# The GELU between the expert layers: in pieces of two column tiles instead of four

## The chip, the core and the metric

The kernel runs on one NeuronCore of a Trainium2 chip. Its engines are TensorE (PE; its weight loads are listed as PEld), VectorE (DVE), ScalarE (ACT) and GpSimd (POOL); the SP queue issues most DMAs. The metric is the device time of one execution in microseconds, as the median of the runs.

## The reference

The input x has 4 sequences of 2048 tokens with 512 features. It is normalised, and the sum of three things is returned: x, a self-attention over the normalised tokens, and a mixture of experts over them.

```python
xn = _layernorm(x, axis=-1)
# attention: 16 heads of 32
qkv = jnp.einsum('bnc,dc->bnd', xn, qkv_w) + qkv_b
attn = softmax(q @ k^T * HEAD_DIM ** (-0.5))
attention = einsum('bnc,dc->bnd', attn @ v, proj_w) + proj_b
# experts: the two best of 8 for each sequence, by its first token
_, idx = jax.lax.top_k(xn[:, 0, :] @ Wr + br, 2)
h = jnp.einsum('bsd,bkde->bkse', xn, W1[idx]) + b1[idx]
h = jax.nn.gelu(h, approximate=False)
o = jnp.einsum('bkse,bkef->bksf', h, W2[idx]) + b2[idx]
out = x + attention + jnp.sum(o, axis=1) / 2
```

All of it is float32. This is shortened: reshapes and the split into heads are left out.

## The kernel before

**Units.** The attention is cut into 1024 units. A unit U is one block of 128 keys against one chunk of 512 queries, for a group of four heads; 16 units are a chunk, four chunks a group, four groups a sequence. A unit opens with the `shift` matmuls (L725), which put the negative row maxima into four PSUM banks, and goes on with the scores on top of them (`score`, L733). Between these stand the plain scores of a unit that comes 22 units later (`score_max`, L715), of which VectorE takes maxima (L855). ScalarE then takes Exp of the four score tiles into a `p` tile (L849), and GpSimd adds the `p` tiles up (`add_weights`, L762 and L766; the last of a chunk by an adding DMA, L764). An even unit also has the product of the last two `p` tiles with v (`weigh`, L745). All PSUM tiles come from one ring of 8 banks (`bank`), so a tile waits until the tile eight places before it has been read. The `p` tiles come from a ring of 4.

**Dense work.** The linear layers are cut into items, and an odd unit takes one item behind its scores: `qk` and `v` projections, `w1` and `w2` of the experts, and `proj`. `dense` emits an item; most have 32 matmuls (`product`, L485). Twenty-two further units ahead of unit 0, with negative numbers, hold the first `v` items and the first `w1` items.

**The experts.** The first layer is done for two chunks of tokens at a time with seven products of half-size blocks in place of eight, each for two halves of the columns (q = 0, 1). The order of the products in `w1` items is `GAPS`: (1,0); (1,1); (6,0),(6,1); (7,0),(7,1); (5,0),(3,0); (5,1),(3,1); (4,0),(4,1); (2,0),(2,1). `combine` adds each into the tiles `hT[0]` (the even chunk) and `hT[1]` (the odd chunk), of 128 partitions by four column tiles of 512. Columns 2q and 2q+1 of `hT[1]` are complete with product (3,q), those of `hT[0]` with (2,q). Eight `w2` items follow, four blocks of 128 tokens that read `hT[1]`, then four that read `hT[0]`. There are 16 such passes: 4 sequences, 2 pairs of chunks, 2 experts.

**The GELU.** It is done in place, by one ScalarE instruction over a whole `hT` tile, in the unit two after the item that completes it. `dense` notes it in `curves` under that unit's number, and the unit's loop takes it behind its four Exps:

```python
curve = curves.pop(U, None)
if curve is not None:
    flat = curve.rearrange("p f n -> p (f n)")
    nc.scalar.activation(flat, flat, AF.Gelu)
```

In the unit that holds a GELU, `dense` is told so (`on_dve`), and `combine` then copies a first product with VectorE instead of ScalarE.

**The planner.** `Plan` gives every odd unit its item ahead of time: fixed ones (`qk`, `v`) at places written out by hand, the others from queues in order. Some odd units stay empty; candidates are those at place 5 of a chunk, and one is left empty whenever the share owed is above zero, unless it would hold a GELU (`curve` in the planner). Loads on SP are placed from the items' units; `keys_at` makes the sum over GpSimd's totals one unit later where place 5 is empty.

Of the kernel before, what the change touches and what calls it, by code (L numbers as in the profile page):

```python
# [37 lines left out]
class Plan:  # L38
# [6 lines left out]
    def __init__(self, B, DC, NCH, NT, TPC):  # L45
# [13 lines left out]
        for G in range(1, B * DC):  # L59
            b, g = divmod(G, DC)  # L60
            first = (G - 1) * self.per_group
            for n, products in enumerate(GAPS):
                at = (11, 12, 13, 14, 15, 16, 17, 19) if g else (5, 6, 7, 8, 9, 11, 12, 13)
                fixed[first + 2 * at[n] + 1] = ("qk", b, g, products)
            if g == 0:
                at = [n for n in range(14, 32) if n % 8 != 2]
# [10 lines left out]
        for b in range(1, B):  # L77
            q1 = (b - 1) * self.per_seq + self.per_group
            q2 = q1 + self.per_group
            for k in range(TOP_K):  # L80
                at = q1 + ((NT - 1, q2 - q1 + 5 * NT - 1) if b > 1 else (-1, NT - 1))[k]
# [4 lines left out]
            for n in range(NT):  # L86
                self.extra.setdefault(q1 + 2 * (16 + n) + 1, []).append(("stats", b, n))
                c, i = divmod(n, TPC)
                at = q2 + 2 * (1 + 18 * (c // 2) + 5 * (c % 2) + i) + 1
# [3 lines left out]
            for p in range(NCH // 2):  # L93
                at = q2 + 2 * NT * (p + 1) - 1
# [46 lines left out]
        current, before, owed = [], None, 0  # L141
        for s in slots:
            if s in fixed:
                self.items[s] = [fixed.pop(s)]
                before = None
                continue
            curve = before is not None and before[0] == "w1" and before[4][-1] in ((3, 1), (2, 1))
            before = None
            if s in rests:
                owed += share  # L150
                if owed > 0 and not curve:
                    owed -= 1
                    continue
            if not current:
                for queue in (proj, ffn):
                    if queue and queue[0][0] <= s:
                        current = queue.pop(0)[1]
                        break
            if current:
                before = current.pop(0)  # L160
                self.items[s] = [before]
# [77 lines left out]
def block_kernel(  # L239
# [37 lines left out]
    def bank(name):  # L277
        return ps.tile([P, CH], F32, tag="bank", name=name)
# [202 lines left out]
    def product(pp, terms, last=True, first=True):  # L481

        for n, (lhsT, rhs) in enumerate(terms):
            for j in range(GH):
                nc.tensor.matmul(  # L485
                    pp[rows_of(j), :], lhsT[:, rows_of(j)], rhs,
                    start=(first and n == 0), stop=(last and n == len(terms) - 1),
                )

    kT, qT = {}, {}  # L490
    hT, bias, b1s = {}, {}, {}
# [16 lines left out]
    def project_v(b, n, xn, w, U):  # L508

        c, i = divmod(n, TPC)  # L510
        pp = bank(f"vps_{b}_{n}")
        product(pp, [(xn[:, d, ts(i, P)], w[:, d, :]) for d in range(DC)])
        t = pair.tile([P, D], F32, tag="vrow", name=f"v_{b}_{n}")
        nc.vector.tensor_tensor(t, pp, bv_bc, ALU.add)
        later(U + 2, lambda: nc.sync.dma_start(v_dram[b, c][:, i, :], t))

    def combine(i, x, c, b1, b2, on_dve):

        add = nc.vector.tensor_tensor
        biased = nc.vector.scalar_tensor_tensor  # L520
        if i == 1 and on_dve:
            nc.vector.tensor_copy(c[0, 0], x)
        elif i == 1:
            nc.scalar.activation(c[0, 0], x, AF.Identity)  # L524
        elif i == 6:
            add(c[0, 1], x, c[0, 0], ALU.add)
        elif i == 7:
            add(c[1, 0], x, c[0, 1], ALU.add)
        elif i == 5:
            biased(c[1, 1], x, b2, c[1, 0], ALU.add, ALU.add)  # L530
            add(c[0, 1], x, c[0, 1], ALU.add)
        else:
            at, b_ = {3: ((0, 1), b1), 4: ((1, 0), b2), 2: ((0, 0), b1)}[i]
            biased(c[at], x, b_, c[at], ALU.add, ALU.add)
# [29 lines left out]
    def blocks(kind, b, n, U):  # L564
# [10 lines left out]
        else:  # L575
# [4 lines left out]
            if n == 3:  # L580
                later(U + (2 if b == 0 else 4), lambda: nc.sync.dma_start(ws_dram[b, k], raw))

    outs = {}

    def dense(item, U, on_dve, between):
        kind, b = item[:2]
        tiles = [held[n] for n in plan.needs(item)]
        if kind == "qk":
            g, products = item[2:]
            for n, (i, p) in enumerate(products):  # L590
                wt, xt = tiles[2 * n : 2 * n + 2]
                pp = bank(f"qkps_{b}_{g}_{i}_{p}")
                product(pp, [(wt[:, d, 0, :], xt[:, d, :]) for d in range(2)])
                o = outs.setdefault((b, g, p), {})
                where = {1: (0, 0), 6: (0, 1), 7: (1, 0), 5: (1, 1)}.get(i)
                if where is not None:
                    c = 2 * p + where[1]
                    t = "kq"[where[0]]
                    o[where] = (kT if t == "k" else qT)[b, g, c] = kv_pool.tile(
                        [P, CH], F32, tag=t, name=f"{t}T_{b}_{g}_{c}",  # L600
                        bufs=2 * NCH if t == "k" else NCH + 3,
                    )
                combine(i, pp, o, bqkv[:, DC + g : DC + g + 1], bqkv[:, g : g + 1], on_dve)
                if n == 0:
                    between()
        elif kind == "v":
            n = item[2]
            project_v(b, n, tiles[1] if b else stage[0, n // TPC], tiles[0], U)
        elif kind == "w1":
            p, k, products = item[2:]  # L610
            for n, (i, q) in enumerate(products):
                wt, xt = tiles[2 * n : 2 * n + 2]
                if (i, q) in ((1, 0), (6, 0)):
                    cc = int(i == 6)
                    hT[cc] = stream.tile(
                        [P, DC, CH], F32, tag="h", name=f"h_{b}_{p}_{k}_{cc}", bufs=2
                    )
                pp = bank(f"hps_{b}_{p}_{k}_{i}_{q}")
                product(pp, [(wt[:, d, q, :], xt[:, d, :]) for d in range(2)])
                o = {(r, cc): hT[cc][:, 2 * q + r, :] for r in range(2) for cc in hT}  # L620
                cols = [b1s[b, k][:, 2 * q + r : 2 * q + r + 1] for r in range(2)]
                combine(i, pp, o, *cols, on_dve)
                if n == 0:
                    between()
                if (i, q) in ((3, 1), (2, 1)):
                    at = U + 2 if U > 0 or U == -1 else U + 1
                    curves[at] = hT[i == 3]
        elif kind == "w2":
            p, c, k, i = item[2:]
            w, row = tiles  # L630
            pp = bank(f"ops_{b}_{c}_{k}_{i}")
            product(pp, [(hT[c % 2][:, f, ts(i, P)], w[:, f, :]) for f in range(DC)])
            nc.vector.scalar_tensor_tensor(row, pp, 0.5, row, ALU.mult, ALU.add)  # L633
            later(U + 2, lambda: nc.sync.dma_start(part_dram[b, c, i], row))
        else:
            qc, i = item[2:]
            at, w, row = tiles
            pp = bank(f"prps_{b}_{qc}_{i}")
            product(pp, [(at[:, g, ts(i, P)], w[:, g, :]) for g in range(DC)])
            finish(b, qc, i, pp, row, U)  # L640

    def finish(b, qc, i, pp, row, U):
        tok = qc * CH + i * P
        nc.vector.tensor_tensor(row, pp, row, ALU.add)  # L644
        later(U + 2, lambda: nc.sync.dma_start(out[b, tok : tok + P, :], row))
# [49 lines left out]
    def place(u):  # L695
        rest, kt = divmod(u, NT)
        rest, qc = divmod(rest, NCH)
        return (*divmod(rest, DC), qc, kt)

    mx, negm, sacc, psums, sums, pT = {}, {}, {}, {}, {}, {}  # L700
    curves, waiting, ends = {}, {}, []

    def later(u, do):
        waiting.setdefault(u, []).append(do)
# [124 lines left out]
    for U in range(-LEAD, plan.units):  # L829
# [20 lines left out]
        curve = curves.pop(U, None)  # L850
# [13 lines left out]
        before = place(U - NT)[:3] if U >= NT else None  # L864
# [30 lines left out]
        for step, sb, n in plan.extra.get(U, []):  # L895
# [10 lines left out]
            else:  # L906
                c, i = divmod(n, TPC)
# [6 lines left out]
        for item in plan.items.get(U, []):  # L914
            dense(item, U, curve is not None, invert if two else lambda: None)
# [28 lines left out]
    U = plan.units  # L944
# [18 lines left out]
    for i in range(TPC):  # L963
        q = ts(i, P)
# [52 lines left out]
```

## Time and profile before

| | |
|---|---|
| median of 3 runs | 5038.61 us (5038.29 to 5046.06) |
| the profiled execution | 5042.55 us, span 5040.8 us |
| TensorE busy | 4947.0 us, 98% of the span, clock 0.997 |
| GpSimd busy | 4429.2 us, 88% |
| VectorE busy | 3740.2 us, 74% |
| ScalarE busy | 2394.0 us, 47% |
| GELU | 32 of 1.91 us |
| table loads on ScalarE | 71 of 1.28 us: 32 ahead of a GELU, 35 ahead of an Exp, 4 ahead of a square root |

Busy shares are averages over the whole execution. TensorE's matmuls overlap, and their ends are modelled, so that single instructions of about 0.6 us stand closer together than their durations say. The names in the rows are those of the program: `p`, `h` (the `hT` tiles), `s` and `m` (scores), `acc` (product with v). "<-" in square brackets names what ended the idle time before an instruction. A row of several instructions has the time from the first one's start to the last one's end.

### The profile page before, as it was taken

To read this page: it belongs to the slowest core of one execution; us is meant where nothing else is said; L and a number is where in the kernel's file an instruction comes from. 1 tells how busy PE (TensorE), PEld (TensorE's weight loads), DVE (VectorE), ACT (ScalarE), POOL (GpSimd) and SP (SyncE) were. 2 spreads that over 40 slices of the span, in tenths; PEclk is the share of its full clock that TensorE was granted. 3 is DMA by queue.
4 is the path that set the end of the run, shared out by engine and by line. 5 is a ranking of instruction groups with operands and counts; after the bars stand their busy time and mean duration, and the time that the engine had idled before them with its cause. 6 is when DMAs were issued, how large, how long until landed. Compare 5 with 4: busy or idle time off the path is not lost. (4 is left out here: it accounts for less than half of the span.)

```text
span 5040.8 us, 107883 instructions
## 1 busy us (share of the span) xinstructions
PE 4947.0 (98%) x45028; PEld 1725.8 (34%) x45028; DVE 3740.2 (74%) x5909; ACT 2394.0 (47%) x4406; POOL 4429.2 (88%) x1498
## 2 busy tenths in 40 slices
PE   8999999999999999999999999999999999999998
PEld 2333333333333333333333333333333333333332
DVE  5777887777777788777777777877777777777762
ACT  1445445454444545454444444555444445454453
POOL 2799998999898998999889998999988988999981
PEclk9999999999999999999999999999999999999999
DMA  6333334433233434434224234434423343323312
GB/s 219 111 103 117 115 96 127 142 122 109 80 107 104 126 107 122 140 114 141 89 86 125 85 121 118 146 122 136 134 70 106 100 123 101 101 80 101 107 62 95
DMA packets 297128, 568.16 MB, mean 113 GB/s; under 512 B 24636, under 2 KB 144188, under 8 KB 279744
## 3 DMA queue, kind: packets, MB, share of 16 engines
q1 hardware_dynamic: 287568, 495.19, 29.4%
q0 software_dynamic: 9072, 66.06, 6.7%
q8 instruction: 354, 5.80, 0.5%
q14 instruction: 134, 1.10, 0.1%
HBM read 367.44 MB, written 127.66 MB: 98 GB/s over the span
## 5 line engine op out<-in xcount | busy, mean ns | idle before, releaser
L766 POOL TENSOR_TENSOR psum<-psum,p 128x2048 f32<-128x2048 f32 x819 | 3722.4, 4545 | 167.6 <-ACT p L849 129.2
L849 ACT ACTIVATE p<-s 128x512 f32<-128x512 f32 x4096 | 2118.0, 603 | 2364.9 <-PE m L715 2181.8
L855 DVE TENSOR_REDUCE mx<-m 128x1 f32<-128x512 f32 x4096 | 2544.2, 684 | 570.1 <-PE m L715 569.8
L733 PE MATMUL s<-qT,kT 32*128 32x512 f32 x8192 | 1919.1, 588 | 0.0
L715 PE MATMUL m<-kT,qT 32*128 32x512 f32 x8192 | 1911.3, 590 | 6.4 <-ACT h L524 3.4
L715 PEld LDWEIGHTS m<-kT,qT 32*128 32x128 f32 x8192 | 920.9, 184 | 334.9 <-issue 244.7
L745 PE MATMUL acc<-p,v 128*32 128x512 f32 x8192 | 988.5, 600 | 37.0 <-ACT p L849 37.0
L733 PEld LDWEIGHTS s<-qT,kT 32*128 32x128 f32 x8192 | 768.6, 185 | 29.2 <-issue 7.3
L485 PE MATMUL ops<-wb_w,h 128*32 128x512 f32 x4096 | 466.0, 595 | 0.6 <-ACT p L849 0.2
L745 PEld LDWEIGHTS acc<-p,v 128*32 128x32 f32 x8192 | 214.2, 109 | 737.0 <-ACT p L849 420.5
L762 POOL TENSOR_TENSOR psum<-p,p 128x2048 f32<-128x2048 f32 x63 | 287.5, 4563 | 203.2 <-ACT p L849 203.2
L754 DVE TENSOR_TENSOR sacc<-acc,sacc 128x512 f32<-128x512 f32 x448 | 309.9, 692 | 158.3 <-PE acc L745 158.3
L485 PE MATMUL hps<-xt,wt_w 128*32 128x512 f32 x3584 | 411.0, 596 | 2.5 <-ACT p L849 2.0
L725 PE MATMUL s<-negm,ones_b 32*128 32x512 bf16 x4096 | 405.7, 385 | 6.2 <-ACT p L849 5.9
L485 PE MATMUL qkps<-xt,wt_qk 128*32 128x512 f32 x3360 | 387.8, 599 | 9.8 <-ACT p L849 9.2
L725 PEld LDWEIGHTS <-ones_b 32*128 32x128 bf16 x4096 | 103.2, 91 | 858.2 <-issue 858.1
L870 DVE RECIPROCAL sums<-sums 128x128 f32<-128x128 f32 x252 | 237.6, 943 | 0.7 <-ACT sums L784 0.7
L485 PEld LDWEIGHTS ops<-wb_w,h 128*32 128x32 f32 x4096 | 120.0, 109 | 308.6 <-issue 229.8
L633 DVE SCALAR_TENSOR_TENSOR row<-ops,row 128x512 f32<-128x512 f32 x128 | 88.4, 691 | 170.3 <-PE ops L485 116.3
L485 PE MATMUL prps<-wb_proj,xl_at 128*32 128x512 f32 x1792 | 203.9, 595 | 0.3
L485 PEld LDWEIGHTS hps<-xt,wt_w 128*32 128x32 f32 x3584 | 103.3, 109 | 268.2 <-issue 186.1
L485 PEld LDWEIGHTS qkps<-xt,wt_qk 128*32 128x32 f32 x3360 | 97.3, 110 | 273.9 <-issue 181.6
(123 smaller groups left out, 1981.6 us busy)
## 6 DMA issues: line engine op xcount, KB each, us to landing
xt<-t_dram SPq DMA_DIRECT2D x181, 512.0 KB, 4.3
xt<-xn_dram SPq DMA_DIRECT2D x133, 512.0 KB, 5.0
psum<-p POOLq DMA_DIRECT2D x63, 1024.0 KB, 8.2
part_dram<-row SPq DMA_DIRECT2D x128, 256.0 KB, 2.0
v_dram<-v SPq DMA_DIRECT2D x64, 256.0 KB, 2.7
wt_w<-ws_dram SPq DMA_DIRECT2D x128, 128.0 KB, 3.3
v<-v_dram SPq DMA_DIRECT2D x64, 256.0 KB, 4.9
row<-in_x_dram SPq DMA_DIRECT2D x64, 256.0 KB, 6.5
```

The costliest lines, as they stand in the source:

```text
L485: nc.tensor.matmul(pp[rows_of(j), :], lhsT[:, rows_of(j)], rhs, start=(first and n == 0), stop=(last and n == len(terms) - 1),)
L633: nc.vector.scalar_tensor_tensor(row, pp, 0.5, row, ALU.mult, ALU.add)
L715: nc.tensor.matmul(t, qT[b, g, qc][r, ts(i, P)], kT[b, g, kc][r, :], start=True, stop=True)
L725: nc.tensor.matmul(tiles[j], ones_b[r, :], negm[b, g, qc][r, :], start=True, stop=False)
L733: nc.tensor.matmul(tiles[j], kT[b, g, kt // TPC][r, ts(kt % TPC, P)], qT[b, g, qc][r, :], start=False, stop=True,)
L745: nc.tensor.matmul(acc[r, :], held["v", (b, g, kt // TPC)][:, (kt + n) % TPC, r], pT[u + n][:, j, :], start=(n == 0), stop=(n == 1),)
L754: nc.vector.tensor_tensor(t, acc, t, ALU.add)
L762: nc.gpsimd.tensor_tensor(psums[b, g, qc], pT[u - 1], pT[u], ALU.add)
L766: nc.gpsimd.tensor_tensor(psums[b, g, qc], psums[b, g, qc], pT[u], ALU.add)
L849: nc.scalar.activation(pT[U][:, j, :], tiles[j], AF.Exp, scale=SCALE)
L855: nc.vector.tensor_reduce(dst, t, AX.X, ALU.max, negate=True)
L870: nc.vector.reciprocal(sums[before][:, q], sums[before][:, q])
```

## The change

The GELU over a whole `hT` tile becomes two, each over two of its four column tiles, and each in an odd unit of its own. For `hT[1]` the first piece is noted when product (3,0) is done and the second when (3,1) is done. For `hT[0]` both are noted when (2,1) is done, for the next two odd units. The planner's condition for not leaving a unit empty is widened to the units that now hold a piece.

```diff
-            curve = before is not None and before[0] == "w1" and before[4][-1] in ((3, 1), (2, 1))
+            curve = before is not None and (
+                before[0] == "w1" and before[4][-1] in ((3, 0), (3, 1), (2, 1))
+                or before[0] == "w2" and before[3] % 2 == 1 and before[5] == 0
+            )
...
+    def following(U):
+
+        return U + 2 if U >= -1 else U + 1
...
-                if (i, q) in ((3, 1), (2, 1)):
-                    at = U + 2 if U > 0 or U == -1 else U + 1
-                    curves[at] = hT[i == 3]
+                if i == 3:
+                    curves[following(U)] = hT[1][:, 2 * q : 2 * q + 2, :]
+                if (i, q) == (2, 1):
+                    curves[following(U)] = hT[0][:, :2, :]
+                    curves[following(following(U))] = hT[0][:, 2:, :]
```

## The prediction

> **What bounds the kernel now.** I read the page first (busy shares and groups), then the groups with shapes kept apart, then the timeline around a GELU, on ScalarE and on TensorE, and last the waits. Times are us, of one profiled execution.
>
> The page and its groups: which engine is full, and what the GELU consists of.
>
> ```profile
> PE 4947.0 (98%) x45028; PEld 1725.8 (34%) x45028; DVE 3740.2 (74%) x5909; ACT 2394.0 (47%) x4406; POOL 4429.2 (88%) x1498
> ...
> L766 POOL TENSOR_TENSOR psum<-psum,p 128x2048 f32<-128x2048 f32 x819 | 3722.4, 4545 | 167.6 <-ACT p L849 129.2
> L849 ACT ACTIVATE p<-s 128x512 f32<-128x512 f32 x4096 | 2118.0, 603 | 2364.9 <-PE m L715 2181.8
> ```
>
> TensorE has work 98% of the time, so whatever lets it stand still is paid in full. ScalarE is idle half the time: its busy time is not what a GELU costs. The GELU's own rows, from the groups of the whole trace:
>
> ```profile
> L853 ACT ACTIVATE h<-h 128x2048 f32<-128x2048 f32 x32 | 61.2, 1912 | 0.4
> L849 ACT ACT_TABLE_LOAD x35 | 44.9, 1283 | 25.6 <-PE m L715 25.5
> L853 ACT ACT_TABLE_LOAD x32 | 41.1, 1283 | 0.6
> ```
>
> There are 32 GELUs of 1.91, and each is a detour: a load of the GELU's table before it (L853), and a load of Exp's table before the next Exp (L849; 3 of the 35 follow square roots). The L853 loads wait for next to nothing; those of L849 wait 25.5 in total for TensorE.
>
> One GELU on ScalarE, from the timeline (start, duration, engine, line, operation, idle before and releaser):
>
> ```profile
> 1718.64 2.07 ACT L849 ACTIVATE p<-s 128x512 f32<-128x512 f32 x4 [2.09 <-PE m L715]
> 1720.72 1.28 ACT L853 ACT_TABLE_LOAD   x1
> 1722.02 1.91 ACT L853 ACTIVATE h<-h 128x2048 f32<-128x2048 f32 x1
> 1724.24 1.28 ACT L849 ACT_TABLE_LOAD   x1 [0.31 <-PE m L715]
> 1725.53 2.07 ACT L849 ACTIVATE p<-s 128x512 f32<-128x512 f32 x4
> 1729.38 2.07 ACT L849 ACTIVATE p<-s 128x512 f32<-128x512 f32 x4 [1.78 <-PE m L715]
> ```
>
> And TensorE in the even unit that follows (L725 opens a unit, L745 is its product with v):
>
> ```profile
> 1722.91 0.39 PE L725 MATMUL s<-negm,ones_b 32*128 32x512 bf16 x4
> ...
> 1726.18 1.92 PE L745 MATMUL acc<-p,v 128*32 128x512 f32 x16 [1.16 <-ACT p L849]
> ...
> 1728.04 0.40 PE L725 MATMUL s<-negm,ones_b 32*128 32x512 bf16 x4
> ```
>
> The reader should see three things. First, the GELU's table load starts at 1720.72, right behind the odd unit's last Exp, and the GELU ends at 1723.93: all of it lies beside the odd unit's dense product (TensorE busy to 1722.91) and the next unit's scores. Second, Exp's table load does not follow the GELU at once. It starts at 1724.24, which is 1.33 after the unit opened. An Exp without a table load starts 1.34 after its unit opens (1729.38 against 1728.04). So the load stands behind the Exp's wait for the first scores, and its whole 1.28 falls after them. Third, TensorE then has no PSUM bank for L745 until the first Exp empties one, and is idle 1.16. The unit lasts 5.12 instead of 3.90 (one without a GELU before it: 501.41 to 505.31): 1.22 lost.
>
> That the load waits for the scores, and not for the GELU, is seen best where ScalarE has something else behind the GELU, a normalisation (L441):
>
> ```profile
> 847.55 1.28 ACT L853 ACT_TABLE_LOAD   x1
> 848.85 1.91 ACT L853 ACTIVATE h<-h 128x2048 f32<-128x2048 f32 x1
> 850.66 0.80 ACT L441 ACTIVATE xl_normal<-xl_normal,nb,sd 128x512 f32<-128x512 f32 x1
> 851.66 1.28 ACT L849 ACT_TABLE_LOAD   x1 [0.19 <-PE m L715]
> ```
>
> That unit opened at 850.33, so the load again starts 1.33 later, though the GELU had ended at 850.76, 0.90 before. Read at each of the 32 GELUs, the load starts 1.32 to 1.33 after the unit opens in 29, while their gap behind the GELU lies between 0.31 and 0.91. The 32 units behind a GELU lose 43.0 over 3.90 each: 32 x 1.22 = 39.0, and 4 more in a few where work for a new chunk or slow GpSimd sums come on top.
>
> **The change part by part.** *Removed:* 32 GELUs of 128x2048. Each held ScalarE 1.91 beside covered work. *Added:* 64 of 128x1024. Exact length unknown: at least half of 1.91 (0.96) if nothing is fixed, at most 1.91; the small rows of ScalarE (128x512 at 0.60 to 0.83) put it near 1.06. Which value is right doesn't matter. The half GELU would end some 0.85 earlier, about 1.7 before Exp's load may start at all, instead of 0.31. I count a gain of 0; what hides it is the odd unit's product and the scores. If the load could follow the GELU at once, there would be a gain, and that is the first rival.
>
> *Added, table loads:* 32 for GELU and 32 for Exp. The GELU's 1.28 starts behind the odd unit's last Exp and ends before the next unit's scores, as now: 0. Exp's 1.28 is the exposed one: 1.22 of TensorE each. Every GELU is in an odd unit and followed by an even one, so the new stalls have the place and the size of the old: 64 x 1.22 = 78.1 against 39.0, **+39.0**. The bounds for a new stall are 0 (if it falls where TensorE waits for something else anyway) and 1.6 (the longest idle before L745 behind a GELU now); I take 1.22, since 28 of 32 have the same idle of 1.16 ahead of L745.
>
> The Trainium skill speaks against this change. "ScalarE: Activation LUTs", section "Rules for kernel authors", says to do all of one table set before switching to another; "What ACT_TABLE_LOAD costs" there prices a switch at about 1283 ns plus about 1380 ns of drain, 2.66 in all. The trace has the 1283, but no drain: the load starts 0.01 after the last Exp (1720.71 to 1720.72), and the Exp 0.01 after its load. By the page, 64 new switches make 170 on ScalarE, and if half of them, Exp's, stood on the path, +85. By the row it is 1.22 for the exposed switch and 0 for the other. I take the row, which includes all that really followed a switch.
>
> *Moved:* pieces of GELU. For the odd chunk (hT[1]) the first piece goes to the unit of products (5,1),(3,1), two units earlier than before, and the second stays in that of (4,0),(4,1). For the even chunk the first stays in the unit of the first w2 block, the second goes to the second block. First readers: hT[1] is read by the first w2 block, four units after its second piece; hT[0] by the fifth, well after. So no product waits longer. GELU issues no DMA, and nothing of SP or GpSimd is passed. The half at (5,1),(3,1) runs while VectorE writes the other half of the same tile; if dependencies hold per slice, no one waits. A start-up row speaks for slices: TensorE turns the first slice of x while ScalarE still writes the later ones.
>
> ```profile
> 12.84 2.93 ACT L441 ACTIVATE x<-x,nb,sd 128x512 f32<-128x512 f32 x4 [0.85 <-POOL nb L437]
> 13.71 2.42 PEld L455 LDWEIGHTS xt<-ident,x 128*128 128x128 f32 x12 [6.11 <-ACT x L441]
> ```
>
> *Queued behind the new pieces on ScalarE:* normalisations in four of the new GELU units, 0.80 each. A half GELU ends near 5.8 after its unit opens, so the normalisation ends at 6.6, still ahead of the scores at 5.61 + 1.33 = 6.94. Cost 0. The Exps behind a load come 1.27 late, and with them GpSimd's sum of that unit. It runs 13.81 without a break over the example's stall, so it is still working off earlier units: 0. VectorE has 1.41 idle in the stalled unit: 0.
>
> *The planner:* three empty odd units (slots 53, 661, 901) now would hold a GELU piece, so each moves to the next such slot, 16 units later, and the dense items between come one odd unit earlier, with their loads on SP. The number of empty units is unchanged, and the instructions and DMAs too: 0, with a bound of 1 either way for each. The choice of engine for the copy of the first product (VectorE in a GELU unit) changes nowhere, since no first product falls into a new GELU unit.
>
> *Given back:* GpSimd, 88% busy, at times falls behind, and then Exp waits for a p buffer; the waits show it as
>
> ```profile
> ACT p L849 <- DMA psum<-p: 36.3, 9, 7.4
> ```
>
> Over the timeline, TensorE is idle 19.8 in 14 units at the third or fourth place of a chunk for this reason. A new stall shortly before lets GpSimd catch up. Six of these units have new GELUs in the 30 units before them, and at 1.22 for each such GELU and no more than is there it makes at most about 6. I take -2.
>
> *Sum:* +39.0 - 2 = +37. The profiled execution took 5042.55 (span 5040.8 and 1.75 around it), so it would be 5079.6; that execution is 3.9 above the median of the three runs (5038.61). Against the median: **5075.6**, +0.73%.
>
> **The rivals.** *The shorter GELU frees Exp's load (faster).* Place: the gap between GELU and Exp's table load. If the load were held by the GELU's end and could run before the scores, a half GELU would end at 5.8 after its odd unit opens, the load at 7.1, 1.45 after the even unit opened (5.61), so Exp is 0.12 late and not 1.27: 64 x 0.12 = 8 instead of 43, -35, about 5004. It decides from the point at which the load doesn't wait for TensorE. For it: loads and GELU fill ScalarE almost up to the scores, so the stall looks like one of length. Against: the gap, 0.31 to 0.91 at the same 1.33.
>
> *GpSimd's lag takes the stalls in.* If all 19.8 came back: +19, about 5058. For: GpSimd is second at 88%. Against: most of that lag sits away from new GELUs.
>
> *Writes wait for whole tiles.* VectorE's writes of (5,1) would wait for the half GELU, which ends at 5.8 of its unit, 1.8 behind the first product (16 matmuls from 2.05 on, 1.9 long). The queue holds 3.1 there (L530 0.74, L531 0.68, a reciprocal 0.94, L534 0.73), then the next unit's maxima, 1.9 late, of which the 1.22 stall covers part: 0.7 to 1.9 x 16 = 11 to 30 more, 5087 to 5106. Against: the slice row above.
>
> **How the numbers follow.** Chances: the stall per GELU 0.85, the freed load 0.04, GpSimd's relief 0.04, whole tiles 0.04. The load freed in about half of the cases is left 0.03; it alone ends within 0.2% (10 us, about what a measurement of this kernel tells from no change). Slower 0.93, same 0.03, faster 0.04. The range starts at 5065 (39 less twice the possible 6 of relief) and ends at 5087 (three planner moves, a few stalls of 1.6, and the 7.8 between the runs shown).
>
> **What would show it.** Right: 64 GELUs near 1.06, 64 table loads at L853 and 67 at L849; Exp's load still 1.33 after its unit opens, with a gap of about 1.2 behind the GELU; about 74 of idle ahead of L745 behind GELUs instead of 38; TensorE's busy time unchanged. Wrong: Exp's load right behind the half GELU, or even units behind a GELU under 4.5; or VectorE idle for ScalarE at L530 in the units of (5,1),(3,1).

## The result, and the profile after

The changed kernel takes 5079.66 us (median of 6 runs) against 5039.14 before, a ratio of 1.0074 (95% interval 1.0063 to 1.0086): slower by 40.5. The profiled executions, on which the readings below rest, have spans of 5078.3 and 5040.8, 37.5 apart.

The page after the change, and its groups for ScalarE and for TensorE's product with v (lines have moved on by 9: L858 is the Exp, L862 the GELU, L754 the product with v):

```profile
PE 4950.4 (97%) x45028; PEld 1731.8 (34%) x45028; DVE 3740.3 (74%) x5909; ACT 2482.9 (49%) x4502; POOL 4429.3 (87%) x1498
...
L754 PE MATMUL acc<-p,v 128*32 128x512 f32 x8192 | 987.6, 600 | 71.3 <-ACT p L858 71.3
```

```profile
L858 ACT ACT_TABLE_LOAD x67 | 86.0, 1283 | 90.6 <-PE m L724 88.7 <-issue 1.8
L862 ACT ACT_TABLE_LOAD x64 | 82.1, 1283 | 1.1
L862 ACT ACTIVATE h<-h 128x1024 f32<-128x1024 f32 x64 | 67.7, 1058 | 0.7
```

TensorE has the same number of matmuls and 3.4 more of busy time; the other 34.1 of the 37.5 is idle time. The wait ahead of the product with v, which went from 37.0 to 71.3, makes up all of it. The granted clock is 0.997 in both executions, so it does not explain the difference. On ScalarE, 64 GELUs of 1.06 take 67.7 where 32 took 61.2, and there are 64 more table loads. The idle time ahead of Exp's loads went from 25.6 to 90.6: each half GELU is done earlier, and ScalarE then stands idle until it may load the table.

One piece on ScalarE, in the same two units whose timeline was shown of before (the even unit opens at 1724.82):

```profile
1720.55 2.06 ACT L858 ACTIVATE p<-s 128x512 f32<-128x512 f32 x4 [2.09 <-PE m L724]
1722.63 1.28 ACT L862 ACT_TABLE_LOAD   x1
1723.93 1.06 ACT L862 ACTIVATE h<-h 128x1024 f32<-128x1024 f32 x1
1726.15 1.28 ACT L858 ACT_TABLE_LOAD   x1 [1.16 <-PE m L724]
1727.44 2.07 ACT L858 ACTIVATE p<-s 128x512 f32<-128x512 f32 x4
```

The gap behind the GELU is 1.16 where it was 0.31: the 0.85 that the GELU became shorter is all in it. The load starts 1.33 after the unit opens, as before. TensorE in that even unit:

```profile
1724.82 0.40 PE L734 MATMUL s<-negm,ones_b 32*128 32x512 bf16 x4
...
1728.09 1.92 PE L754 MATMUL acc<-p,v 128*32 128x512 f32 x16 [0.90 <-ACT p L858]
1729.95 0.40 PE L734 MATMUL s<-negm,ones_b 32*128 32x512 bf16 x4
```

The product with v starts 3.27 after the unit opens, as in the stalled unit of before, and the unit lasts 5.13. Here 0.90 of it is shown as idle; of the 64 units behind a piece, 54 have 1.15 or 1.16. All last at least 5.11, against 3.90 for an even unit without.

Why the load waits can be seen too. Here are the rows of the Exp's line around that load, counted by kind (shortest, median and longest duration in ns, then first and last start):

```profile
L858 ACTq EVENT_SEMAPHORE  x1: 17/17/17, 1726.1 to 1726.1; - x1
L858 ACT ACT_TABLE_LOAD  x1: 1283/1283/1283, 1726.1 to 1726.1; - x1
```

In front of the load stands a wait instruction (EVENT_SEMAPHORE) of the same line. It is the one for TensorE's scores: the load's idle time above ends by TensorE. In one unit the instruction behind the GELU is a square root (L437), whose own wait comes after its load, and that load does start at once; it is the square root that then waits:

```profile
1995.00 1.06 ACT L862 ACTIVATE h<-h 128x1024 f32<-128x1024 f32 x1
1996.08 1.28 ACT L437 ACT_TABLE_LOAD   x1
1998.39 0.22 ACT L437 ACTIVATE sd<-sd 128x16 f32<-128x16 f32 x1 [1.02 <-DVE sd L436]
```

### The profile page after: what moved, and what is told of

Same layout as the page of the kernel before. It is cut to its first block, busy times and chain, and to the rows that moved or that the text cites. A ratio compares the mean times of both kernels' runs of the same rounds, so it can differ in the third digit from the quotient of the medians.

```text
span 5078.3 us, 107974 instructions
## 1 busy us (share of the span) xinstructions
PE 4950.4 (97%) x45028; PEld 1731.8 (34%) x45028; DVE 3740.3 (74%) x5909; ACT 2482.9 (49%) x4502; POOL 4429.3 (87%) x1498
## 5 line engine op out<-in xcount | busy, mean ns | idle before, releaser
L858 ACT ACTIVATE p<-s 128x512 f32<-128x512 f32 x4096 | 2118.1, 603 | 2246.6 <-PE m L724 2070.2
L864 DVE TENSOR_REDUCE mx<-m 128x1 f32<-128x512 f32 x4096 | 2544.2, 684 | 568.2 <-PE m L724 567.9
L754 PE MATMUL acc<-p,v 128*32 128x512 f32 x8192 | 987.6, 600 | 71.3 <-ACT p L858 71.3
L754 PEld LDWEIGHTS acc<-p,v 128*32 128x32 f32 x8192 | 215.1, 109 | 771.7 <-ACT p L858 455.9
```

The costliest lines, as they stand in the source:

```text
L754: nc.tensor.matmul(acc[r, :], held["v", (b, g, kt // TPC)][:, (kt + n) % TPC, r], pT[u + n][:, j, :], start=(n == 0), stop=(n == 1),)
L858: nc.scalar.activation(pT[U][:, j, :], tiles[j], AF.Exp, scale=SCALE)
L864: nc.vector.tensor_reduce(dst, t, AX.X, ALU.max, negate=True)
```

## The experiments

The theory, S in the expectations: each return to Exp's table costs one stall of about 1.2, since its load stands behind the wait for the scores; neither the GELU's length nor the number of pieces matters. Rivals: ScalarE's added busy time (L), a cost of the pieces or of the moved empty units as such (P). Each ratio is to the kernel before, run beside it on the same chip.

**Free the load.** A tiny Exp of a constant behind each GELU, so that the load belongs to an instruction that waits for nothing; with the pieces, and with the whole GELU.

```diff
+    warm = const.tile([P, 8], F32, name="warm")
+    nc.gpsimd.memset(warm, 0.0)
...
             nc.scalar.activation(flat, flat, AF.Gelu)
+            nc.scalar.activation(warm[:, 4:], warm[:, :4], AF.Exp)
```

> The changed kernel, with a tiny Exp (128x4, of a constant tile, result unused) right behind every GELU piece, so that Exp's table load need not stand behind the real Exp's wait for the scores. Theory S (each GELU costs one stall of 1.22, because Exp's load waits for the scores): the load starts within 0.1 of the GELU's end, 5.8 after the odd unit opened, ends at 7.1, the tiny Exp at 7.3, the first real Exp some 0.3 late instead of 1.27; 64 stalls of about 0.25 instead of 1.22, so about 5018 (5008 to 5026), below the kernel before. Rival L (ScalarE's added busy time, 89 us, is what costs): ScalarE gets 64 instructions more, so 5080 to 5095. Rival P (the pieces as such cost: the waits of VectorE or TensorE on parts of a tile, or the moved empty units): no change, 5075 to 5085.

> The kernel before, with the same tiny Exp behind each of its 32 whole GELUs. Theory S: the GELU ends 6.63 after its odd unit opened, so the load ends at 7.9, the tiny Exp at 8.1, and the first real Exp is still 1.0 to 1.2 late against 1.27: 32 x 0.1 to 0.3 less, 5029 to 5037. With the load free, the length of the GELU does matter, which is why pieces should gain far more from this than whole GELUs. Rivals L and P: 5039 to 5045.

Measured: with pieces 5023.49 (0.9965, 0.9951 to 0.9979), with whole GELUs 5039.58 (0.9994, 0.9985 to 1.0003). The pieces with the tiny Exp on ScalarE:

```profile
1706.03 1.28 ACT L864 ACT_TABLE_LOAD   x1
1707.33 1.06 ACT L864 ACTIVATE h<-h 128x1024 f32<-128x1024 f32 x1
1708.39 1.28 ACT L865 ACT_TABLE_LOAD   x1
1709.68 0.20 ACT L865 ACTIVATE warm<-warm 128x4 f32<-128x4 f32 x1
1709.80 2.04 ACT L860 ACTIVATE p<-s 128x512 f32<-128x512 f32 x4
```

The load now starts with the GELU's end, 1.16 earlier than above. Idle behind the 64 pieces adds up to 9.3, against 71.6. ScalarE does 64 instructions more than in the changed kernel, and the run is 56 faster: L falls, and P with it. With whole GELUs the load starts 1.02 to 1.03 after the unit opens in 20 of 32 cases instead of 1.32, and the idle behind the 32 is 31.7 instead of 37.9. The time of that run can't be told from before, and at 5039.58 it missed its range of 5029 to 5037. So a shorter GELU pays, but only once the load follows the GELU.

**Take the switch away, keep the pieces; shorten the GELU, keep the switches.** The first kernel has Identity for GELU, which leaves the GELU out; the second leaves half of the columns without it.

In the changed kernel:

```diff
-            nc.scalar.activation(flat, flat, AF.Gelu)
+            nc.scalar.activation(flat, flat, AF.Identity)
```

> The changed kernel with Identity in place of GELU (this leaves the GELU out of the computation): the same 64 pieces in the same units, with no table load around them. Theory S: all 64 stalls go, 5080 - 78 = 5002 (4993 to 5008). Rival P: the costs of the 32 GELUs of before go, those of the pieces as such stay, 5036 to 5046.

In the kernel before:

```diff
-            nc.scalar.activation(flat, flat, AF.Gelu)
+            nc.scalar.activation(flat[:, : 2 * CH], flat[:, : 2 * CH], AF.Gelu)
```

> The kernel before, where each of the 32 GELUs takes only the first 1024 of its 2048 columns (the others keep their values without GELU): half the length, as many switches. Theory S: a shorter GELU only lengthens the gap ahead of Exp's load from 0.31 to about 1.16; same time as before, 5034 to 5044. Rival of length (the stall is ScalarE's GELU and loads being too long for the unit): 0.85 less in each of 32 stalls, 27 less, about 5012.

Measured: Identity 5014.34 (0.9944, 0.9927 to 0.9961), half the columns 5040.94 (1.0002, 0.9993 to 1.0011). Half the columns, on ScalarE:

```profile
1720.06 1.28 ACT L853 ACT_TABLE_LOAD   x1
1721.35 1.06 ACT L853 ACTIVATE h<-h 128x1024 f32<-128x1024 f32 x1
1723.57 1.28 ACT L849 ACT_TABLE_LOAD   x1 [1.16 <-PE m L715]
1724.87 2.07 ACT L849 ACTIVATE p<-s 128x512 f32<-128x512 f32 x4
```

A GELU half as long, in the place of the whole one, saves nothing: the rival of length, that foresaw 27 less, falls. With Identity the 64 pieces cost TensorE 1.8 in all. But the run came out some 12 above the 5002 foreseen, outside its range of 4993 to 5008. Its idle at places 2 and 3 of the chunks (counted from 0), away from GELUs, is 27.3, where it was 19.8 before (19.8 to 22.2 in the traces with 32 stalls from whole or halved GELUs and all of GpSimd's sums), with a single unit of 5.8; the waits of ScalarE name GpSimd's sums and their DMA:

```profile
ACT p L858 <- DMA psum<-p: 46.1, 10, 7.8
...
ACT p L858 <- POOL psum L775: 23.4, 7, 3.8
```

Before, these were 36.3 and 8.9. The last pair of runs below takes this up.

**Parts of the change alone.** Two halves in one unit, in the kernel before:

```diff
             flat = curve.rearrange("p f n -> p (f n)")
-            nc.scalar.activation(flat, flat, AF.Gelu)
+            for n in range(2):
+                piece = flat[:, 2 * n * CH : 2 * (n + 1) * CH]
+                nc.scalar.activation(piece, piece, AF.Gelu)
```

> The kernel before, with each whole GELU issued as two halves back to back in the same odd unit: 64 GELU instructions, but still 32 switches there and 32 back. Theory S (one stall for each return to Exp's table): same time as before, 5034 to 5046; GELU and its load end 6.84 after the unit opened, just ahead of the scores. Rival P (pieces as such cost, some 0.6 each for 64): 5075 to 5085.

Only the odd chunk in two units, in the changed kernel:

```diff
                 if (i, q) == (2, 1):
-                    curves[following(U)] = hT[0][:, :2, :]
-                    curves[following(following(U))] = hT[0][:, 2:, :]
+                    curves[following(U)] = hT[0]
```

> The changed kernel with only the odd chunk's GELU in two pieces; the even chunk's stays whole in one unit: 48 GELUs, 48 returns to Exp's table. Theory S: 16 stalls of 1.22 more than before, +20, half of the change: 5061 (5053 to 5067). If the late piece of the even chunk were what costs (rival P2), 5041; if writing the other half of the tile during its first piece were (P3), 5080.

Only the planner's part, in the changed kernel:

```diff
-                if i == 3:
-                    curves[following(U)] = hT[1][:, 2 * q : 2 * q + 2, :]
-                if (i, q) == (2, 1):
-                    curves[following(U)] = hT[0][:, :2, :]
-                    curves[following(following(U))] = hT[0][:, 2:, :]
+                if (i, q) in ((3, 1), (2, 1)):
+                    curves[following(U)] = hT[i == 3]
```

> The changed kernel's planner (three empty odd units moved 16 units on) with GELU whole and in the units of before. Theory S: 5035 to 5047, no difference from before beyond 5. Rival (the moved empty units cost): over 5050.

Measured: halves in one unit 5044.74 (1.0002, 0.9994 to 1.0011), odd chunk only 5062.34 (1.0036, 1.0023 to 1.0049), planner only 5044.67 (1.0003, 0.9995 to 1.0012), beside 5042.97 for the kernel before. Sixty-four GELU instructions with 32 switches cost what 32 cost:

```profile
1719.74 1.28 ACT L855 ACT_TABLE_LOAD   x1
1721.04 2.00 ACT L855 ACTIVATE h<-h 128x1024 f32<-128x1024 f32 x2
1723.26 1.28 ACT L849 ACT_TABLE_LOAD   x1 [0.22 <-PE m L715]
```

With 48 switches the loss is 0.36%, about half of the change's 0.74%, and the idle behind GELUs is 52.9, against 37.9 with 32 and 71.6 with 64. So the loss goes with the number of returns to Exp's table. The moved empty units are not seen in the time.

**A version that beats both.** With the load free, the length counts, so three pieces of a third each, with the tiny Exp behind each, 96 GELUs.

```diff
-                before[0] == "w1" and before[4][-1] in ((3, 0), (3, 1), (2, 1))
-                or before[0] == "w2" and before[3] % 2 == 1 and before[5] == 0
+                before[0] == "w1" and before[4][-1] in ((3, 0), (3, 1), (4, 1), (2, 1))
+                or before[0] == "w2" and before[3] % 2 == 1 and before[5] < 2
...
-                if i == 3:
-                    curves[following(U)] = hT[1][:, 2 * q : 2 * q + 2, :]
-                if (i, q) == (2, 1):
-                    curves[following(U)] = hT[0][:, :2, :]
-                    curves[following(following(U))] = hT[0][:, 2:, :]
+                ends_ = (0, 684, 1366, 2048)
+                at = U
+                for n in {(3, 0): (0,), (3, 1): (1, 2), (2, 1): (0, 1, 2)}.get((i, q), ()):
+                    at = following(at)
+                    flat = hT[i == 3].rearrange("p f n -> p (f n)")
+                    curves[at] = flat[:, ends_[n] : ends_[n + 1]]
...
-            flat = curve.rearrange("p f n -> p (f n)")
-            nc.scalar.activation(flat, flat, AF.Gelu)
+            nc.scalar.activation(curve, curve, AF.Gelu)
+            nc.scalar.activation(warm[:, 4:], warm[:, :4], AF.Exp)
```

> Three pieces of 684, 682 and 682 columns for each tile, each in an odd unit of its own with the tiny Exp behind it: 96 GELUs. Theory S, with the load freed: the piece of about 0.76 ends at 5.5, load and tiny Exp at 7.0, so the first real Exp is on time within 0.1 and the 9 of idle that the run with two pieces and the tiny Exp still has behind GELUs goes to about 0 to 3. GpSimd's lag takes some of it back, as in the run with Identity (5014), so 5012 to 5022 and no better than that run. Rival L (each further table load costs something on its own, in any place): above 5030.

Measured: 5018.69 (0.9951, 0.9938 to 0.9965), 24 below the kernel before beside it. Its interval overlaps that of the two pieces with the tiny Exp, so those two can't be told apart by time. One piece of it on ScalarE:

```profile
1721.90 1.28 ACT L864 ACT_TABLE_LOAD   x1
1723.20 0.77 ACT L864 ACTIVATE h<-h 128x682 f32<-128x682 f32 x1
1723.99 1.28 ACT L865 ACT_TABLE_LOAD   x1
1725.28 0.20 ACT L865 ACTIVATE warm<-warm 128x4 f32<-128x4 f32 x1
1725.87 2.06 ACT L861 ACTIVATE p<-s 128x512 f32<-128x512 f32 x4 [0.39 <-PE m L727]
```

The tiny Exp is done 0.39 before the scores arrive, so the real Exp is on time. There are 192 table loads around the pieces, and the idle behind all 96 is 3.0. Of the rest that could be had, GpSimd's lag keeps some: 27.0 of idle at places 2 and 3.

**Who took back part of the gain.** One of GpSimd's sums left out per chunk, in the kernel before and in the run with Identity. The row sums of the softmax then miss one block of keys.

```diff
-        if kt == 0 or u >= plan.units - NT:
+        if kt in (0, 14) or u >= plan.units - NT:
```

> The kernel before, with one of GpSimd's sums of p tiles left out in each chunk (place 14; so the row sums of the softmax miss one block of keys): 4.55 less for GpSimd per chunk. It is the control for the next run. Theory G (GpSimd's lag makes the 19.8 of idle at places 2 and 3 of chunks): most of that idle goes, 5020 to 5032. If that idle has another cause: 5036 to 5046.

> The run with Identity in place of GELU, with the same sum left out as in the control. With GELU's stalls gone, idle at places 2 and 3 was 27 instead of 20. Theory G: GpSimd's lag took back part of the gain; with the lag out of the way the run lies 43 (35 to 46) below the control instead of 27 below before, so about 4985 (4978 to 4995). If something else took it back: only some 27 below the control.

Measured: 5015.44 (0.9947, 0.993 to 0.9964) for the control, 5 below the expected range, and 4980.51 (0.9878, 0.9862 to 0.9895) with Identity. The idle at places 2 and 3 falls to 4.6 and 5.0, so that idle was GpSimd's lag. The two runs are 34.9 apart, at the lower edge of the 35 to 46 expected, and their idle behind GELUs differs by 35.6 (37.9 and 2.3): with the lag away, nearly all of the stalls comes back as time. The 43 foreseen is the whole length that the 32 units had lost, with chunk work and slow sums in it.

With the lag there, the gain was 27, 8 less. Not all of the 8 is the lag. TensorE's busy time and the granted clock also moved; these are the rows of the run with Identity, of the control and of Identity with the sum left out:

```profile
PE 4953.9 (99%) x45028; PEld 1727.2 (34%) x45028; DVE 3739.7 (75%) x5909; ACT 2312.9 (46%) x4375; POOL 4431.2 (88%) x1498
PE 4940.2 (99%) x45028; PEld 1725.5 (34%) x45028; DVE 3737.6 (75%) x5909; ACT 2394.4 (48%) x4406; POOL 4144.5 (83%) x1435
PE 4938.1 (99%) x45028; PEld 1725.4 (35%) x45028; DVE 3736.6 (75%) x5909; ACT 2312.7 (46%) x4375; POOL 4144.8 (83%) x1435
```

The same matmuls took 4947.0 before. The granted clock was 0.997 there, 0.995 in the first of these rows and 0.998 in the other two. The first row is also the slowest of its four runs (5021.25). At like clocks the gain of Identity is about 30: 5014.3 (two runs) against 5044.8 (nine) at 0.996, and 5010.9 (one run) against 5040.5 (fourteen) at 0.997. So, as an estimate from few runs, the lag kept some 5 of the 8 and the clock the rest; the remaining 4 of the 12 are the step from the 39 foreseen to 35. The clock may also be why the control came out 5 below its range: 6.8 of its gain lies in TensorE's busy time. Why the clock differs between these kernels stays open.

## Why the prediction was right, and where it was off

*The stall per return, +39.0: right in mechanism and nearly in size.* It measured +37.0. Thirty-three units are newly stalled and last 37.2 longer than before; one is no longer stalled (an item moved by the planner), -1.2; those stalled in both traces last 1.0 longer together. The difference to 39.0 is in ten of the new ones. They had lasted 4.05 to 4.68 before, not 3.90, and last 5.12 after, so that they lost 0.4 to 1.1 instead of 1.22, 3.5 less together. The step "every new stall has the size of the old" took 3.90 as the length without a stall everywhere.

*GpSimd gives back, -2: not there.* All other units together are 0.4 longer. The idle at places 2 and 3 is 20.0 after and 19.8 before: 37 of added stalls did nothing for the lag. In the opposite direction it moved: with the stalls removed this idle was 24.3 to 27.3, against 19.8 to 22.2 in the traces with 32 of them. That the sum came out so close is partly luck: the term of -2 had no effect behind it, and the ten cheaper stalls, which the working did not see, happened to make up for it.

*The GELU's shorter length, 0: right.* The piece takes 1.06, as estimated; the 0.85 saved lies in the gap, and half the columns with as many switches moved nothing. One figure of the working is off: the half GELU was said to end about 1.7 before Exp's load may start, but 0.31 and 0.85 make 1.16, which is what was measured. Nothing else rested on it. The first rival, the freed load, was the right account of what would happen if the load could follow the GELU, as the tiny Exp showed: 5023.49 where its figure was 5004. Its residue of 8 was met (9.3 of idle behind the pieces). But of the 35 it foresaw, 18 came (5041.15 before). The idle behind GELUs fell by 28.6, less than 35, and the idle at places 2 and 3 rose by 4.5, to 24.3. At a like clock of 0.996 the gain is 22 (5022.6, mean of four runs, against 5044.8, mean of nine), so some 4 go with the clock. The small rest was not split further.

*The switch to GELU, 0, and no drain: right.* The L862 loads wait 1.1 in total. The price of 2.66 per switch in the Trainium skill, "ScalarE: Activation LUTs", section "What ACT_TABLE_LOAD costs", gave an estimate of +85 with half of the switches on the path; the change costs 40. With 96 pieces and freed loads, 192 table loads leave 3.0 of idle, so that page's rule to do all of one table set before switching (section "Rules for kernel authors") cost nothing to break here, where the switches fit beside other work.

*The planner, 0: right*, 1.0003 alone. *VectorE waiting for whole tiles: not seen.* In the trace after the change none of VectorE's waits ahead of the `h` tiles names ScalarE; all name TensorE. Its idle time ahead of the mx maxima is 568.2 against 570.1, and with Identity the pieces left 1.8 of idle.

*The sum.* +37 foreseen, +37.5 between the profiled executions, +40.5 between the medians, with an interval of about 32 to 43. That the profiled execution of before lay 3.4 above the median and that of after 0.4 makes the difference between the last two.

## What to carry to other kernels

Before making an instruction shorter, look at what the next one waits for: here the idle time behind the GELU, constant against another engine's start and not against the GELU's end, said that its length was worth nothing and that each further piece would pay nearly the full table load. Where a table load stands behind its activation's wait, a tiny activation of the same function, put right behind the foreign one, takes the load off the path; only then is it worth cutting the foreign one to the size of the hole. And a gain on the fullest engine can be partly kept by the second fullest, here some 5 of 35: see how far behind it already is.

## What the runs showed of the hardware that was not expected

In these traces a table load stands right ahead of its activation, behind any separate wait instruction and ahead of the activation's own wait. Exp's load starts behind a separate wait instruction for the scores, 1.31 to 1.33 after the unit opens in 62 of 64 cases, while a square root's load in the same queue, at 1996.08, started 0.02 after the GELU's end, and the square root itself waited afterwards. Two loads, a GELU of 682 columns and a tiny Exp take 3.58 together, with 0.02 or less between load and activation: a change of table and back costs ScalarE 2 x 1.28 and nothing more that these traces show.

The granted clock followed neither TensorE's busy share nor the chip alone. It was 0.998 in all eight runs with one GpSimd sum less per chunk, and 0.996 or 0.997 in seven runs of the kernel before beside them; with Identity or the tiny Exp in the pieces, and all of GpSimd's sums, it was 0.995 to 0.997. In the 24 runs of the kernel before beside those, 0.001 of clock went with about 4 us (5044.8 at 0.996, 5040.5 at 0.997).
